# Square feed-forward layers as seven half-size products instead of eight

## The chip, the cores and the metric

The kernel runs on one core of a Trainium2 chip. Its time is the device time of one execution in microseconds (us); three runs of the kernel before gave 1289.44, 1290.35 and 1290.55, so the median is 1290.35. The core has TensorE (PE: matmuls, with PEld for its weight loads), VectorE (DVE), ScalarE (ACT), GpSimd (POOL) and SyncE (SP), each with its own queue of instructions that it runs in order; semaphores join them. SBUF is the on-chip memory, PSUM the small memory into which TensorE accumulates, in banks of 128 x 512 fp32.

## The reference

A transformer block on x of shape (4, 1024, 256), all fp32. Cut to what matters:

```
x = x + layernorm(attention(layernorm(x)))          # 16 heads of 16
n = layernorm(x)
h = silu((n @ w1.T) * s1) * ((n @ w2.T) * s2)       # 256 -> 1024, the gated layer
h = gelu((h @ h1.T) * t1)                           # 1024 -> 1024, square
h = gelu((h @ h2.T) * t2)                           # 1024 -> 1024, square
x = x + layernorm((h @ w3.T) * s3)                  # 1024 -> 256, the last layer
```

The weights of the feed-forward part hold only -1, 0 and 1, with one scale per output. The activations are fp32. The kernel keeps that accuracy by splitting each activation into a high part that TensorE's faster fp32r form represents exactly and a low part, the rest; the weights are exact in that form, so a product takes two matmuls, one for each part.

## The kernel before

The program is written with its order by hand: the order in which Python records instructions is the order in each engine's queue. `tile_fast` first runs attention for the four batches. Its main loop (`while weighed < len(tiles)`, L1015) records score matmuls (L473), exponentials on ScalarE (L474) and weighted sums (L481), and between them calls `side.take()`. `Side` (L606) holds chains of `Step`s, each with a gap in slots and a flag for whether it uses TensorE; one `take` is one slot, in which every chain's next due steps are recorded, at most one of them on TensorE. Normalisations, transposes, projections, loads, and the rounding of weights are such steps.

`round_weights` (L246) has GpSimd load a block of weights, cast it to fp32r and write it back to DRAM; 22 blocks in all, 16 of them of h1 and h2. Later `load_weights` (L757) brings h1 into eight tiles that the attention's stacks held (`homes["h1"]`), and h2 and w3 into tiles that come free with the attention. They stay there for the whole feed-forward stage.

`feed_forward` (L947) goes over eight half batches of 512 tokens. For each:

- `gated` (L818): per block of 128 outputs eight matmuls (`pg`, L816), SiLU on ScalarE (L830), the product on VectorE (L832), a split into high (ScalarE, L820) and low (VectorE, L821), and a `side.take()` every second block.
- `gelu_layer` (L840), once for h1 and once for h2: per pair of output blocks, 32 matmuls (`ph`, L816) over eight input blocks, with a `side.take()` after every second one; then GELU (ScalarE, L852), the high part (VectorE, L853) and the low part (VectorE, L854).
- `finish` (L856): the last layer (`pz`, L869) and a chain of side steps that normalises, adds x and stores. VectorE normalises (`Norms.apply`, L114); GpSimd computes the reciprocal root (`Norms.root`, L106). For the last half batch this is recorded in place and not as side steps.
- `prepare` (L784): side steps that normalise and transpose the next half batch's rows.

`check_weights` and `count` (L918) load the weights again and compare them with the rounded ones, in 44 pieces of 128 x 512; `judge` (L932) sums the misses with a small matmul, and if there are any, the slower `tile_general` runs. PSUM is used as three pairs of banks (`ps`, tag `big`), one bank for the attention's sums and one (`misc`) for small work.

## Time and profile before

| what | us |
|---|---|
| median of three runs | 1290.35 |
| the profiled execution, its own time | 1287.27 |
| its span, first to last instruction | 1285.4 |
| TensorE busy in the span (96%) | 1237.9 |
| VectorE busy (57%) | 728.2 |
| ScalarE busy (54%) | 699.9 |
| GpSimd busy (9%) | 121.3 |
| first `pg` matmul of the feed-forward stage, from the span's start | 611.36 |

Matmuls are pipelined and their ends are modelled, so TensorE's busy time counts overlaps: a `ph` matmul reads as 390 ns, while the next starts about 227 ns after it. How often matmuls start is what counts. Groups are given by line, engine, operation and tile, with busy time, mean length of one, and the idle time of the engine just ahead of them with what ended it.

### The profile page before, as it was taken

To read this page: it belongs to the slowest core of one execution; us is meant where nothing else is said; L and a number is where in the kernel's file an instruction comes from. 1 tells how busy PE (TensorE), PEld (TensorE's weight loads), DVE (VectorE), ACT (ScalarE), POOL (GpSimd) and SP (SyncE) were. 2 spreads that over 40 slices of the span, in tenths; PEclk is the share of its full clock that TensorE was granted. 3 is DMA by queue.
4 is the path that set the end of the run, shared out by engine and by line. 5 is a ranking of instruction groups with operands and counts; after the bars stand their busy time and mean duration, and the time that the engine had idled before them with its cause. 6 is when DMAs were issued, how large, how long until landed. Compare 5 with 4: busy or idle time off the path is not lost.

```text
span 1285.4 us, 21095 instructions
## 1 busy us (share of the span) xinstructions
PE 1237.9 (96%) x8104; PEld 767.9 (60%) x8104; DVE 728.2 (57%) x1625; ACT 699.9 (54%) x855; POOL 121.3 (9%) x166
## 2 busy tenths in 40 slices
PE   7999999999999999998999999999999999999995
PEld 3333333333333334333788888888888888888885
DVE  3566566865677647655653635538356374463533
ACT  4788788888888888998412414214132141331410
POOL 6211021110111110000000000000000000000000
PEclk9999999999999999999999999999999999999998
DMA  5776654566465654563310000201102011020000
GB/s 139 175 181 164 152 121 133 117 159 145 117 165 120 152 136 79 100 161 111 133 62 1 25 1 1 74 17 42 49 1 71 20 42 49 1 67 9 17 1 20
DMA packets 65679, 107.03 MB, mean 83 GB/s; under 512 B 12960, under 2 KB 39200, under 8 KB 65568
## 3 DMA queue, kind: packets, MB, share of 16 engines
q1 hardware_dynamic: 57680, 80.93, 25.4%
q0 software_dynamic: 7360, 24.12, 6.1%
q8 instruction: 66, 1.08, 0.3%
q10 hardware_dynamic: 528, 0.52, 0.1%
q14 instruction: 45, 0.37, 0.1%
HBM read 48.38 MB, written 23.59 MB: 56 GB/s over the span
## 4 chain that ended last, share of the span: by engine, by line
PE 75%; DVE 8%; ACT 8%; DMA 3%; issue 3%; SPq 1%; ACTq 1%; POOL 0%; POOLq 0%; DVEq 0%
PE ph L816 36%; PE acc L481 12%; PE s L473 8%; ACT e L474 6%; PE pz L869 4%; PE pg L816 4%; PE p L267 4%; PE py L267 2%; DVE sg L832 2%; PE pv L267 2%; DVE top L490 1%; DVE ha_lo L821 1%; DVE st L96 1%; PE po L520 1%; SPq L421 1%
## 5 line engine op out<-in xcount | busy, mean ns | idle before, releaser
L474 ACT ACTIVATE e<-s 128x1024 f32<-128x1024 f32 x512 | 482.9, 1037 | 53.7 <-PE s L473 43.8
L481 PE MATMUL acc<-e,vaug 128*32 128x512 f32 x2048 | 255.1, 600 | 2.4 <-POOL vaug L451 2.3
L852 ACT ACTIVATE a<-ph,h_scale 128x512 f32<-128x512 f32 x128 | 81.3, 688 | 301.1 <-PE ph L816 301.1
L473 PE MATMUL s<-sq,sk 64*128 64x512 f32 x1024 | 184.7, 441 | 17.1 <-ACT e L474 13.5
L816 PE MATMUL ph<-hb_hi,h 128*128 128x512 f32 x512 | 199.5, 390 | 0.0
L816 PE MATMUL ph<-hb_lo,h 128*128 128x512 f32 x512 | 199.4, 389 | 0.0
L473 PEld LDWEIGHTS s<-sq,sk 64*128 64x128 f32 x1024 | 85.5, 184 | 137.3 <-ACT e L474 115.0
L490 DVE TENSOR_TENSOR top<-top,e 128x512 f32<-128x512 f32 x192 | 134.9, 702 | 16.0 <-ACT e L474 10.9
L106 POOL TENSOR_TENSOR rstd<-ve,minus_half 128x4 f32<-128x4 f32 (+1 forms) x33 | 38.4, 1162 | 831.5 <-DVE ve L104 831.5
L481 PEld LDWEIGHTS acc<-e,vaug 128*32 128x32 f32 x2048 | 49.1, 108 | 106.9 <-issue 101.8
L816 PEld LDWEIGHTS ph<-hb_hi,h 128*128 128x128 f32 x512 | 96.1, 188 | 20.2
L816 PEld LDWEIGHTS ph<-hb_lo,h 128*128 128x128 f32 x512 | 96.1, 188 | 20.1
L853 DVE CAST ha_hi<-a 128x512 fp32r<-128x512 f32 x64 | 27.1, 423 | 142.7 <-ACT a L852 142.7
L816 PE MATMUL ph<-ha_hi,sq 128*128 128x512 f32 x256 | 101.8, 398 | 0.4
L816 PE MATMUL ph<-ha_lo,sq 128*128 128x512 f32 x256 | 99.8, 390 | 0.0
L816 PE MATMUL ph<-ha_lo,sk 128*128 128x512 f32 x256 | 99.7, 390 | 0.0
L816 PE MATMUL ph<-ha_hi,sk 128*128 128x512 f32 x256 | 99.7, 389 | 0.0
L830 ACT ACTIVATE sg<-pg,w_scale 128x512 f32<-128x512 f32 x64 | 43.4, 690 | 55.9 <-DVE ha_lo L821 45.4
L832 DVE SCALAR_TENSOR_TENSOR sg<-pg,w_scale,sg 128x512 f32<-128x512 f32 x64 | 47.1, 745 | 46.3 <-ACT sg L830 46.2
L267 PE MATMUL p<-xT,wqk_sb 128*32 128x512 f32 x512 | 61.9, 602 | 6.3 <-ACT wqk_sb L194 2.6
L853 DVE CAST hb_hi<-a 128x512 fp32r<-128x512 f32 x64 | 27.0, 422 | 71.5 <-ACT a L852 71.5
L816 PEld LDWEIGHTS ph<-ha_hi,sq 128*128 128x128 f32 x256 | 48.1, 188 | 13.0 <-DVE sg L832 3.4
(165 smaller groups left out, 1636.7 us busy)
## 6 DMA issues: line engine op xcount, KB each, us to landing
w<-in_h_dram POOLq DMA_DIRECT2D x16, 512.0 KB, 5.7
h_r<-wr POOLq DMA_DIRECT2D x16, 512.0 KB, 3.9
x<-in_h_dram SPq DMA_DIRECT2D x32, 256.0 KB, 2.7
top_d<-top SPq DMA_DIRECT2D x30, 256.0 KB, 2.3
folded<-top_d SPq DMA_DIRECT2D x30, 256.0 KB, 3.1
sk<-ck1hi SPq DMA_DIRECT2D x64, 64.0 KB, 2.7
sk<-ck1lo SPq DMA_DIRECT2D x64, 64.0 KB, 3.0
sq<-cq1hi SPq DMA_DIRECT2D x64, 64.0 KB, 2.5
```

Of the source, the lines that this page charges most:

```text
L106: nc.gpsimd.tensor_tensor(rstd[:, :n], ve[:, :n], self.minus_half[:, :n], ALU.pow)
L267: nc.tensor.matmul(o[j : j + SLOT, :], w[:, j : j + SLOT], i, **flags)
L473: nc.tensor.matmul(s[:, a, :], stacks[1, g % 2, u][r, c * P : (c + 1) * P], stacks[0, g % 2, u][r, h * NQ : (h + 1) * NQ], start=True, sto ...
L474: nc.scalar.activation(pair(k)[:, u], s, AF.Exp)
L481: nc.tensor.matmul(acc[SLOT * i : SLOT * (i + 1), :], vaug[g % 2][:, c, i, :], pair(k)[:, i // 2, i % 2, :], start=c == 0, stop=c == NT - 1)
L490: nc.vector.tensor_max(top, top if c > 1 else pair(k - 2)[:, :, :, 0:P], pair(k)[:, :, :, 0:P])
L816: nc.tensor.matmul(p, homes[n][c][:, m * P : (m + 1) * P], half[:, c, :], start=c == 0 and k == 0, stop=c == len(homes[n]) - 1 and k == 1)
L830: nc.scalar.activation(sg, p[:, 0, :], AF.Silu, scale=scales["w1"][:, m : m + 1])
L832: nc.vector.scalar_tensor_tensor(sg, p[:, 1, :], scales["w2"][:, m : m + 1], sg, ALU.mult, ALU.mult)
L852: nc.scalar.activation(a, p[:, j, :], AF.Gelu, scale=scales[n][:, m : m + 1])
L853: nc.vector.tensor_copy(o[0][:, m, :], a)
L869: nc.tensor.matmul(p[t], half[:, c, t * P : (t + 1) * P], homes["w3"][c], start=c == 0 and k == 0, stop=c == HC - 1 and k == 1)
```

## The change

The square layers are now computed for a whole batch (two halves of 512 tokens) by a scheme with seven products of half-size blocks. The weight is a 2 x 2 array of blocks, the activation another (upper or lower 512 features, first or second 512 tokens), and seven products of sums and differences give the four output blocks.

- *Weight side.* `round_corners` takes the place of `round_weights` for h1 and h2: GpSimd copies three corners and forms four sums or differences, and stores seven "factors" per layer to DRAM. `load_factor` brings one factor (1 MB) at a time into a ring of four slots, which are the tiles that held h1.
- *Activation side.* `Operand` splits a block into high (now a ScalarE copy of 128 x 1024) and low (VectorE). `t1`, `make2`, `make3`, `make4` form sums of operands on VectorE.
- *A layer.* `Layer.run` records 14 groups of 16 matmuls, seven products with two pairs of row blocks each. Where one product serves several sums, the partial sum is copied by ScalarE from one pair of PSUM banks to another (`branch`) or to SBUF (`keep_copy`), and matmuls go on accumulating on the copy. Side steps, splits and sums stand in a table by group (`steps`).
- *Around it.* `gated` runs both halves of a batch, 16 blocks, without splits of its own and with a `side.take()` at each; its last steps split and add the first operands of the layer after. `finish` handles both halves. ScalarE normalises (`Norms.scale`, `Norms.shift`) rows of batches after the first and the endings of all batches but the last. The check compares whole blocks of 128 x 1024 with an int8 copy that ScalarE makes, in 22 pieces, and `judge` is recorded just before the last batch's `finish`. The first batch's second half is prepared during attention.

```diff
+    def shift(self, stats, n=TPQ):
+        mv, rstd = stats
+        nb = self.small.tile([P, TPQ], F32, tag="nb", name="nb")
+        self.nc.vector.scalar_tensor_tensor(nb[:, :n], mv[:, :n, 0], -1.0, rstd[:, :n], ALU.mult, ALU.mult)
+        return rstd, nb
+
+    def scale(self, o, t, shifted, i):
+        rstd, nb = shifted
+        self.nc.scalar.activation(o, t, AF.Identity, bias=nb[:, i : i + 1], scale=rstd[:, i : i + 1])
...
+        def round_corners(n, c, x):
+            def load():
+                st["w"] = work.tile([P, WIDE], F32, tag="w", name="w", bufs=1)
...
+                for j in range(2):
+                    nc.gpsimd.dma_start(out=st["w"].rearrange("p (j i n) -> p j i n", j=2, i=2)[:, j], in_=rows[:, j])
...
+            def plain():
+                r = work.tile([P, WIDE], F32R, tag="wr", name="wr", bufs=1)
+                nc.gpsimd.tensor_copy(r[:, 0:half], st["w"][:, 0:half])
+                nc.gpsimd.tensor_copy(r[:, half : 3 * half], st["w"][:, 2 * half : 4 * half])
+                store(r, 0, 3)
+
+            def sums():
+                r = work.tile([P, WIDE], F32R, tag="wr", name="wr", bufs=1)
...
+                nc.gpsimd.tensor_tensor(s1, a21, a22, ALU.add)
+                nc.gpsimd.tensor_tensor(s2, s1.bitcast(F32), a11, ALU.subtract)
+                nc.gpsimd.tensor_tensor(s3, a11, a21, ALU.subtract)
+                nc.gpsimd.tensor_tensor(s4, a12, s2.bitcast(F32), ALU.subtract)
+                store(r, 3, 7)
...
+            return [Step(load, 2, False), Step(plain, 3, False), Step(sums, 1, False)]
...
+        order = (0, 1, 4, 5, 2, 3, 6)
+        def load_factor(q):
...
+            n, k = square[q // len(order) % 2], order[q % len(order)]
+            for i, t in enumerate(ring_of[q % SLOTS]):
+                nc.sync.dma_start(out=t.bitcast(F32), in_=factors[n][k, :, 2 * i : 2 * i + 2, :].bitcast(F32))
...
+            def high(self, i):
+                self.hi[i] = Half("hi", F32R)
+                nc.scalar.copy(self.hi[i].t, self.raw[i].t)
+
+            def low(self, i):
+                self.lo[i] = Half("lo", F32R)
+                nc.vector.tensor_sub(self.lo[i].t, self.raw[i].t, self.hi[i].t.bitcast(F32))
...
+            def run(self, q, scale, extra):
...
+                steps = {
+                    0: [hi(2, 0), self.t1(1), self.make2(1), lo(2, 0)],
+                    1: [hi(2, 1), lo(2, 1), self.make4(0), self.make4(1)],
+                    2: [self.make3(0), self.make3(1), hi(3, 0), lo(3, 0)],
+                    3: [hi(3, 1), lo(3, 1)] + take,
+                    4: [hi(4, 0)] + take + [lo(4, 0)],
...
+                    9: [hi(6, 1)] + take + [lo(6, 1)],
+                    10: take, 11: take,
+                }
...
+                def products(k, r, start):
+                    p = at[r]
+                    for c in range(HC // 2):
+                        for j in range(2):
+                            w = ring_of[(q + k) % SLOTS][c // 2][:, c % 2, (2 * r + j) * P : (2 * r + j + 1) * P]
+                            for n, half in enumerate(self.moving[k].pairs(c)):
+                                nc.tensor.matmul(
...
+                    if r:
+                        self.moving[k].release()
+                        load_factor(q + k + SLOTS)
+
+                def add(n, i, j, r):
+                    o = out[n][r]
...
+                    nc.vector.tensor_add(o.t, at[r], o.t)
+                    gelu(o, i, r)
+
+                def keep_copy(n, r):
...
+                    nc.scalar.copy(o.t, at[r])
...
+                def branch(r):
+                    first[r] = at[r]
+                    nc.scalar.copy(space(r), first[r])
...
+                space(0), products(0, 0, True), branch(0), after(0)
+                space(1), products(0, 1, True), after(1)
+                second(0), branch(1), after(2)
+                products(2, 0, False), keep_copy("u", 0), after(3)
+                second(1), after(4)
+                products(2, 1, False), keep_copy("u", 1), after(5)
+                for g in range(6, 14):
+                    k, r = g // 2, g % 2
...
+                    if k == 3:
+                        keep_copy("w", r)
+                    elif k == 4:
+                        straight(1, r, at[r])
+                    else:
+                        add(*(("w", 1, 1) if k == 5 else ("u", 0, 1)), r)
+                    after(g)
...
+                steps = {g: [side.take] for g in range(NH * HC)}
+                for g, runs in (
+                    (7, opened + split(corner, 0)), (8, split(corner, 1)), (10, split(low, 0)), (11, split(low, 1)),
+                    (12, [one.t1(0)]), (13, [one.make2(0)]), (14, []), (15, []),
+                ):
...
+                two.run(q + 7, scales["h2"], extra)
+                until(lambda: not chain[0])
+                quiet[0] = False
+                if last:
+                    side.flush()
+                    side.add(judge())
+                    side.flush()
+                chain = finish(b, ops, {0: split(ops[0, 1], 0) + split(ops[0, 1], 1)}, [Step(check, 0, False)] if b == 0 else [])
```

## The prediction

> **What bounds the kernel now.** The page comes first: the span, the busy tenths and the granted clock.
>
> ```profile
> span 1285.4 us, 21095 instructions
> ...
> PE   7999999999999999998999999999999999999995
> ...
> DVE  3566566865677647655653635538356374463533
> ACT  4788788888888888998412414214132141331410
> ...
> PEclk9999999999999999999999999999999999999998
> ```
>
> TensorE is 90% busy or more in nearly every slice, at full clock. ScalarE is as busy as TensorE up to slice 20 (the attention, with its exponentials) and idle for most of the second half; VectorE has room throughout. A busy TensorE is not yet a limit, so the chain that ended last, in order of time, is next, over one steady half batch of the feed-forward stage:
>
> ```profile
> 782.61 3.67 PE pg L816 x16
> ...
> 797.32 14.80 PE ph L816 x64
> 812.56 1.86 PE ph L816 x8
> 814.85 41.79 PE ph L816 x184
> 856.64 7.67 PE pz L869 x64
> 864.31 3.67 PE pg L816 x16
> ```
>
> From one `pg` to the next is 81.70 us: 14.71 for the gated layer (64 matmuls), 59.32 for the two square layers (256 matmuls and eight small transposes), 7.67 for the last layer. A matmul in the long run costs 41.79 / 184 = 0.227 us. The groups by form give what the other engines pay:
>
> ```profile
> L474 ACT ACTIVATE e<-s 128x1024 f32<-128x1024 f32 x512 | 482.9, 1037 | 53.7 <-PE s L473 43.8 <-DVE top L490 4.1 <-ACT e L474 2.4
> L852 ACT ACTIVATE a<-ph,h_scale 128x512 f32<-128x512 f32 x128 | 81.3, 688 | 301.1 <-PE ph L816 301.1
> L832 DVE SCALAR_TENSOR_TENSOR sg<-pg,w_scale,sg 128x512 f32<-128x512 f32 x64 | 47.1, 745 | 46.3 <-ACT sg L830 46.2
> L854 DVE TENSOR_TENSOR hb_lo<-a,hb_hi 128x512 fp32r<-128x512 f32 x64 | 44.3, 692 | 2.3
> ```
>
> The GELU (L852) waits for TensorE, not the reverse. So removing matmuls from the square layers shortens the kernel one for one, as long as nothing else gets late. A window of the transfers at the start of the feed-forward (GB/s is the last column) bounds what weight loads can reach:
>
> ```profile
> 640.00:644.00 4.00, 4.00 (x19) 3.32 (x18) 2.43 (x7) 1.27 (x2) 0.00 (x0) 1.00 1.02 414
> ```
>
> **The Trainium skill.** *ScalarE: Activation LUTs*, "What ACT_TABLE_LOAD costs", has an activation at 186 ns + 0.833 ns per element and about 93 ns for each pointer operand. It gives 1039 ns for 1024 elements; the trace has 1037 (L474). *VectorE: DVE Perf Modes*, "The TRN2 errata", has an fp32 tensor_tensor at (N+151)/0.96 ns: 691 for 512, where the trace has 692. *PSUM — Partial Sum Buffer*, "The four PSUM rules", says that writes by ScalarE leave the accumulate bits alone, so a matmul without the first-flag adds to such data where matmuls have written the bank before. The change rests on this; the kernel before never does it, so no trace here shows it. *GPSIMD Engine Reference*, 3.1, has a two-input add at about twice VectorE's time.
>
> **The change, part by part.**
>
> *Matmuls.* Before, a batch (two halves) takes 2 x 256 = 512 matmuls in the square layers. After, a layer is 7 products x 2 row pairs x 16 = 224, so 448 per batch. Removed: 4 x 64 = 256, times 0.227 = **-58.1**. Nothing on TensorE hides that, since it is the chain. The period of 81.70 is 0.5 more than its parts (320 x 0.227 + 7.67 + 0.88 for transposes = 81.2); such seams come half as often: **-2**. The gated and last layers keep their 512 matmuls each.
>
> *Work beside a layer.* A layer now has 14 groups of 3.63 us, 50.8 us. ScalarE, all priced from L474 and L852: 14 splits, 4 kept copies and 2 branch copies at 1.04, 16 GELUs at 0.64 (back to back): 31 us. VectorE: 14 low parts, 8 sums of operands, 4 adds at 1.2 (the skill's 1.22, less overlap): 31 us. With normalisation and checks both stay under 80%, so rates fit and only hand-overs can cost. I followed them in the order of the built program. Branch copy of row pair 0: starts at 3.8, done 4.9, wanted at 7.25. Of row pair 1: behind two GELUs that start at 11.0, done 13.4, wanted at 14.5; queued behind it on ScalarE are splits wanted only at 21.8. The third product wants its last low part at 10.9: t1 and its difference for half 1, then a split and two subtractions, done at about 8.5. These cost nothing, with 1 to 2.5 us of cover.
>
> Two do not fit. The second `w` add of product 6 stands on VectorE behind a low part whose split stands on ScalarE behind two GELUs and four normalisations (0.49 each by the skill's rule with two pointers) or two check casts (1.04 each): done near 47.8 to 48.3, wanted at 47.15. That is 0.7 in three layers and 1.2 in one. With checks at a layer's end the next layer's operand sums start late by some 3 us, and the third product waits up to 2, in three batches: I take 1. Sum **+6**, bounds 0 and 20.
>
> *Gated layer.* Splits, sums and the previous batch's two endings now go into 16 steps of 1.82 us, so VectorE has 26 of 29 us to do. Where statistics and low parts coincide (steps 6 to 12) it falls about 3.5 us behind; the three PSUM buffers give 1.9 of cover (two groups, 3.64, less 1.7 for SiLU and product). 1.5 in three batches, 0.5 in the first: **+5**, bounds 0 and 14.
>
> *Weight factors.* They come from DRAM for each product, 56 loads of 1 MB, two DMAs each on SP's queue. A product lasts 32 x 0.227 = 7.27 us, so 144 GB/s is needed; the window shows 414. A load is issued when its ring slot's product ends and used three products later (22 us); check loads ahead of it on SP may hold it for some 5 us. Cost 0; without that cover it is the second rival below.
>
> *Making the factors.* GpSimd did one 1147 ns cast per block; now two copies and four adds of 256 (0.56 each by the skill's ratio, without start), and two loads and two stores. The second half of a block waits for the first's store (3.9 us to landing before), because one buffer serves both. Behind it in GpSimd's queue stand `rstd` and `vaug`; VectorE waits for `rstd`. TensorE's order in attention is the same up to the last 16 groups. In two places an `rstd` follows closely. **+2**, bounds -1 (a gain is excluded but for the few transposes moved) and 10.
>
> *End.* The final check's matmul now stands between the last product and the last layer, behind an add and a reduction: **+1.8**. In the last batch both halves are normalised in place. The timeline of the end before shows what a block of two tiles costs VectorE:
>
> ```profile
> 1268.43 0.76 DVE L871 TENSOR_TENSOR z<-pz,w3s_sb 128x256 f32<-128x256 f32 x2 [0.72 <-PE pz L869]
> ...
> 1272.91 0.74 DVE L871 TENSOR_TENSOR z<-pz,w3s_sb 128x256 f32<-128x256 f32 x2
> ...
> 1277.04 0.43 DVE L877 TENSOR_TENSOR z<-z,x 128x256 f32<-128x256 f32 x1
> ```
>
> 4.5 us a block against 3.84 of TensorE. Four blocks and two low parts end at 4.0 + 2.4 + 18.1 = 24.5 after the first `pz`, 9.1 after TensorE's last; before it is 5.2. **+4**.
>
> Sum: -58.1 - 2 + 6 + 5 + 2 + 1.8 + 4 = -41.3. On the profiled execution's 1287.27 (span 1285.4 and 1.9 around it) that is 1246.0; the median of the runs shown, 1290.35, is 3.1 above that execution, so **1249**. A difference under 0.2%, 2.6 us, can't be told from none.
>
> **Rivals.**
>
> *All hidden* (chance 0.15). If the hand-overs fit and attention stays, only the check's matmul and the end remain: -60.1 + 5.8 = -54, 1236. For it: both engines have a quarter of their time free. Against: the two places above are late by their order, whatever the mean.
>
> *VectorE and ScalarE set the pace* (0.15). In-order queues can turn 80% load into a late hand-over in most groups. 0.2 us in each of 112 groups is 22 us more: 1271. For it: one late split passes on to adds, GELUs and the next split, across both engines. Against: most steps have over 1 us of cover each 3.6 us, so lateness is worked off.
>
> *The factor stream is late* (0.07), the one that ends slower. Everything saved is gone at 42 us / 56 = 0.75 us more per product, that is at 8.0 us a load or 131 GB/s; at 115 GB/s a product takes 9.1 us and the time is 1249 + 56 x 1.85 = 1353. For it: all loads pass one queue in order, behind stores and checks that wait. Against: 414 GB/s in the window, and 22 us of lead.
>
> *It doesn't do what it says* (0.02): if accumulation onto copied sums needed other matmuls, the count would not fall, and the time is about 1290.
>
> **How the numbers follow.** The main case has 0.61, with its own range 1241 to 1258. Leaving out the lowest tenth (under 1236, most of "all hidden" lies above it) and the highest (beyond 1267: the slower case and the worse part of the pace case) gives 1236 to 1267. Faster: 0.61 + 0.15 + 0.14 = 0.90; within 0.2%: 0.02; slower: 0.08.
>
> **What would show it.** 1792 `ph` matmuls at 0.227, no group of low parts above 1.25, a batch from gated layer to gated layer of 150 to 152 us against 163.4, and 9 us of VectorE after the last `pz`. Idle TensorE on `ph` put down to VectorE adds means the hand-overs, and above 20 us the pace rival; put down to DMA of factors, the stream. The attention ending more than 5 us later than at 611 would make my GpSimd term wrong.

## The result: 1286.7 us for 1289.2

The changed kernel takes 1286.66 us (median of 12 runs, 1283.73 to 1292.07) beside 1289.17 us for the kernel before (12 runs, 1286.14 to 1290.95): a ratio of 0.9985, 95% interval 0.9972 to 0.9999; 0.15%, under the 0.2% that can be told from no change. The prediction was 1249, so of 41 us of expected gain 39 are missing. The profiled execution took 1288.74 us, with a span of 1287.0; before it was 1287.27 and 1285.4.

The matmuls did go. From the page of the changed kernel, the span, the busy times, the granted clock in 40 slices and the chain that ended last; then one of the four groups of `ph` matmuls:

```profile
span 1287.0 us, 20876 instructions
...
PE 1206.6 (94%) x7848; PEld 727.2 (57%) x7848; DVE 823.9 (64%) x1454; ACT 883.0 (69%) x1043; POOL 209.2 (16%) x279
...
PEclk8999899999999999999999999999999999999997
...
PE 60%; ACT 15%; DVE 15%; issue 5%; SPq 2%; DMA 2%; POOL 1%; ACTq 0%; POOLq 0%; DVEq 0%
...
L1014 PE MATMUL ph<-hi,sq 128*128 128x512 f32 x448 | 178.5, 398 | 8.7 <-DVE g L936 5.6
```

4 x 448 = 1792 `ph` matmuls, 256 fewer, as the change says. The chain that ended last read like this on the page of the kernel before:

```profile
PE 75%; DVE 8%; ACT 8%; DMA 3%; issue 3%; SPq 1%; ACTq 1%; POOL 0%; POOLq 0%; DVEq 0%
```

TensorE's share went from 75% to 60%, those of VectorE and ScalarE from 8% to 15% each. Time has moved from multiplying to waiting for one of the other two. TensorE's waits from the first square layer to the end (engine and line, what it waited for, us in total, times, longest):

```profile
PE pn L1187 <- DVE total L1183: 6.6, 1, 6.6
PE fpt L873 <- ACT fxn L123: 5.6, 15, 2.1
PE ph L1014 <- DVE g L936: 5.6, 4, 1.8
PE pz L1121 <- ACT hi L903: 3.4, 3, 1.3
PE ph L1014 <- DVE w L1025: 2.9, 4, 1.3
PE pz L1121 <- DVE lo L907: 2.6, 3, 0.9
PE pg L933 <- DVE g L936: 2.4, 3, 0.8
...
```

Seven kinds (an eighth, of 0.2 us, is left out), few of each, none over 7 us: no single bottleneck, but hand-overs that come late. There are no waits for the weight factors' DMAs among them.

A ledger closes the sum. It takes the distance between the starts of successive matmuls from the first `pg` to the last `pz` in each trace, less what such a matmul takes when nothing is in the way (0.2267 us for `ph` and `pg`, 0.120 for `pz`, 0.108 for a transpose), and sorts the excess by where it falls.

| us, whole feed-forward | before | after | difference |
|---|---|---|---|
| 256 `ph` matmuls at 0.2267 | | | -58.0 |
| `ph` matmuls further apart than 0.2267, with no wait | 1.6 | 9.4 | +7.8 |
| matmuls stretched by a half TensorE clock | 0 | 6.4 | +6.4 |
| waits inside the last layer (`pz`) | 0 | 8.1 | +8.1 |
| the wait for the weight comparison (`pn`) | 0 | 6.8 | +6.8 |
| waits at the transposes (`fpt`) | 0 | 9.0 | +9.0 |
| waits in and behind the gated layer | 1.5 | 10.3 | +8.8 |
| waits between `ph` groups | 0 | 4.4 | +4.4 |
| attention's last projections inside the first gated layer | 0 | 2.0 | +2.0 |
| sum (the rest is under 0.5) | | | -4.7 |

The feed-forward is 4.7 us shorter, the attention in this profile 4.8 longer (the first `pg` at 616.1 after 611.3), and from the last `pz` to the end it takes 1.5 more: 1.6 us more of span. The next three views show how such waits arise.

**Inside the last layer.** Batch 2, first TensorE, then the queues it waits for (start, duration, engine, line, operation; in brackets the idle time before and what ended it):

```profile
935.47 0.28 PE L1121 MATMUL pz<-w_sb,lo 128*128 128x256 f32 x1
937.03 0.38 PE L1121 MATMUL pz<-w_sb,hi 128*128 128x256 f32 x1 [1.28 <-ACT hi L903]
938.29 0.39 PE L1121 MATMUL pz<-w_sb,lo 128*128 128x256 f32 x1 [0.88 <-DVE lo L907]
...
939.80 0.42 PE L1121 MATMUL pz<-w_sb,hi 128*128 128x256 f32 x1
940.02 0.42 PE L1121 MATMUL pz<-w_sb,lo 128*128 128x256 f32 x1
```

```profile
931.18 2.36 DVE L907 TENSOR_TENSOR lo<-w,hi 128x1024 fp32r<-128x1024 f32 x2 [2.34 <-ACT hi L903]
933.46 1.22 DVE L1025 TENSOR_TENSOR u<-ph,u 128x1024 f32<-128x1024 f32 x1
934.59 0.68 DVE L1126 TENSOR_TENSOR z<-pz,w3s_sb 128x512 f32<-128x512 f32 x1
937.01 2.36 DVE L907 TENSOR_TENSOR lo<-u,hi 128x1024 fp32r<-128x1024 f32 x2 [1.74 <-ACT hi L903]
```

```profile
934.71 1.34 ACT L1002 ACTIVATE u<-u,h_scale 128x512 f32<-128x512 f32 x2 [2.62 <-DVE u L1025]
935.95 1.97 ACT L903 CAST hi<-u 128x1024 fp32r<-128x1024 f32 x2
```

The last product had ended at 928.0. Its second add (`u`, 933.46) stands on VectorE behind two low parts of `w`, which wait for their high parts on ScalarE. From the add follow GELU, high part and low part, and the second half of the last layer starts with exactly this block. TensorE has 7.7 us of work for the first half (64 `pz` matmuls) and needs 2.6 more. After the wait the `pz` matmuls start 0.22 us apart instead of 0.12. The windows of the first two batch ends show the granted clock (us, busy of PE, PEld, DVE, ACT and POOL, granted clock, DMA share, GB/s):

```profile
770.00:775.00 5.00, 3.49 (x28) 3.09 (x26) 3.26 (x4) 3.28 (x5) 0.00 (x0) 1.00 0.00 0
775.00:780.00 5.00, 4.72 (x27) 4.72 (x28) 1.96 (x3) 1.22 (x1) 0.00 (x0) 0.66 0.00 0
...
938.00:943.00 5.00, 4.71 (x26) 4.59 (x27) 1.97 (x3) 1.23 (x1) 0.00 (x0) 0.66 0.01 3
```

A clock of 0.66 over 5 us is 3.4 us at one half, and in these 3.4 us 1.1 to 1.6 us of work are lost.

**At the end of the gated layer.** Batch 2, ScalarE and then VectorE:

```profile
808.23 0.69 ACT L935 ACTIVATE sg<-pg,w_scale 128x512 f32<-128x512 f32 x1 [0.19 <-PE pg L933]
813.02 2.08 ACT L123 ACTIVATE z<-z,nb,rstd 128x256 f32<-128x256 f32 x4 [4.10 <-DVE nb L118]
815.01 1.24 ACT L935 ACTIVATE sg<-pg,w_scale 128x512 f32<-128x512 f32 x2
```

```profile
812.83 0.16 DVE L118 SCALAR_TENSOR_TENSOR nb<-mv,rstd 128x4 f32<-128x4 f32 x1 [0.24 <-POOL rstd L108]
...
815.71 0.75 DVE L936 SCALAR_TENSOR_TENSOR g<-pg,w_scale,sg 128x512 f32<-128x512 f32 x1 [1.58 <-ACT sg L935]
```

The four normalisations of the batch before (`z`) stand in ScalarE's queue ahead of the SiLUs (`sg`). ScalarE is idle for 4.1 us, with two SiLUs behind it that could run; VectorE waits for the SiLU, and TensorE for VectorE, because the SiLU products free the PSUM buffers (0.95 us inside the last groups, 1.9 before the first `ph`).

**At the transposes.** ScalarE and TensorE in batch 2:

```profile
862.82 1.33 ACT L1002 ACTIVATE w<-w,h_scale 128x512 f32<-128x512 f32 x2 [2.43 <-DVE w L1025]
864.05 2.06 ACT L123 ACTIVATE fxn<-x,nb,rstd 128x256 f32<-128x256 f32 x4
```

```profile
862.23 0.40 PE L1014 MATMUL ph<-lo,sk 128*128 128x512 f32 x1
864.69 0.33 PE L873 MATMUL fpt<-ident,fxn 128*128 128x128 f32 x1 [2.06 <-ACT fxn L123]
865.18 0.33 PE L873 MATMUL fpt<-ident,fxn 128*128 128x128 f32 x1 [0.16 <-ACT fxn L123]
```

Here the normalised inputs (`fxn`) stand behind two GELUs that wait for an add. TensorE's queue is in order too: all the `ph` matmuls behind the four transposes wait with them.

### The profile page after: what moved, and what is told of

Same layout as the page of the kernel before. It is cut to its first block, busy times and chain, and to the rows that moved or that the text cites. A ratio compares the mean times of both kernels' runs of the same rounds, so it can differ in the third digit from the quotient of the medians.

```text
span 1287.0 us, 20876 instructions
## 1 busy us (share of the span) xinstructions
PE 1206.6 (94%) x7848; PEld 727.2 (57%) x7848; DVE 823.9 (64%) x1454; ACT 883.0 (69%) x1043; POOL 209.2 (16%) x279
## 3 DMA queue, kind: packets, MB, share of 16 engines
q8 instruction: 64, 1.05, 0.3%
## 4 chain that ended last, share of the span: by engine, by line
PE 60%; ACT 15%; DVE 15%; issue 5%; SPq 2%; DMA 2%; POOL 1%; ACTq 0%; POOLq 0%; DVEq 0%
PE ph L1014 22%; PE acc L536 12%; PE s L528 8%; ACT e L529 6%; PE p L322 4%; PE pg L933 3%; DVE lo L907 3%; ACT hi L903 3%; PE pz L1121 3%; PE py L322 2%; SPq L476 2%; DVE g L936 2%; DVE top L545 2%; PE pv L322 1%; ACT w L1002 1%
## 5 line engine op out<-in xcount | busy, mean ns | idle before, releaser
L1014 PE MATMUL ph<-hi,sq 128*128 128x512 f32 x448 | 178.5, 398 | 8.7 <-DVE g L936 5.6
L1014 PE MATMUL ph<-lo,sq 128*128 128x512 f32 x448 | 176.5, 394 | 0.0
L1014 PE MATMUL ph<-hi,sk 128*128 128x512 f32 x448 | 176.3, 394 | 0.0
L1014 PE MATMUL ph<-lo,sk 128*128 128x512 f32 x448 | 176.3, 394 | 0.0
L1014 PEld LDWEIGHTS ph<-hi,sq 128*128 128x128 f32 x448 | 84.2, 188 | 32.5 <-DVE g L936 7.3
L1014 PEld LDWEIGHTS ph<-hi,sk 128*128 128x128 f32 x448 | 84.0, 188 | 19.9
L1014 PEld LDWEIGHTS ph<-lo,sk 128*128 128x128 f32 x448 | 84.1, 188 | 19.8
L1014 PEld LDWEIGHTS ph<-lo,sq 128*128 128x128 f32 x448 | 84.1, 188 | 18.8
L1121 PE MATMUL pz<-w_sb,hi 128*128 128x256 f32 x256 | 67.8, 301 | 3.4 <-ACT hi L903 3.4
L1121 PE MATMUL pz<-w_sb,lo 128*128 128x256 f32 x256 | 67.8, 301 | 2.6 <-DVE lo L907 2.6
```

What stands on the lines that cost most here:

```text
L1014: nc.tensor.matmul(p[:, j, :], w, half, start=start and c == n == 0, stop=c == HC // 2 - 1 and n == 1, skip_group_check=True,)
L1121: nc.tensor.matmul(p[:, j, :D], half[:, (t0 + j) * P : (t0 + j + 1) * P], homes["w3"][c], start=c == n == 0, stop=c == HC - 1 and n == 1,)
```

## The experiments

My theory after the traces: late hand-overs at four places, each with its own remedy, and a half clock that follows from some of them. The rival: VectorE and ScalarE have too much work, so that a wait taken away comes back elsewhere. "Work theory" below is this rival.

| run | median us | ratio to the kernel before, 95% |
|---|---|---|
| changed kernel | 1286.66 | 0.9985 (0.9972 to 0.9999) |
| e1, sums of operands after the gated layer | 1283.80 | 0.9951 (0.9936 to 0.9966) |
| e2, transposes later | 1280.47 | 0.9926 (0.9901 to 0.9950) |
| e3, end of a batch reordered | 1271.38 | 0.9862 (0.9847 to 0.9877) |
| e4, these three | 1263.37 | 0.9796 (0.9779 to 0.9813) |
| e5, `z` normalised later | 1287.03 | 0.9979 (0.9968 to 0.9990) |
| e6, normalising on VectorE | 1271.36 | 0.9862 (0.9835 to 0.9889) |
| e7, e4 and e5, comparison last | 1263.74 | 0.9798 (0.9780 to 0.9816) |
| e9, operands on the weights' alignment | 1279.89 | 0.9930 (0.9908 to 0.9953) |
| e10, the best of all | 1251.33 | 0.9702 (0.9676 to 0.9728) |
| e14, kernel before with 96 bytes moved | 1298.04 | 1.0068 (1.0044 to 1.0091) |

e8, e11, e12 and e13 were run once each, for their traces: 1285.19, 1287.67, 1287.35 and 1289.08 us.

**e1: sums of operands after the gated layer.**

```diff
-                    (12, [one.t1(0)]), (13, [one.make2(0)]), (14, []), (15, []),
...
+                emit([one.t1(0), one.make2(0)])
```

> One edit: the first layer's two sums of operands (t1 and the difference for row pair 0) are issued after the gated layer instead of in its steps 12 and 13. Hand-over theory (VectorE is behind at the end of the gated layer, so its products with the SiLU leave PSUM late, and TensorE waits 0.95 us inside the last groups and 1.9 us before the first ph, in each batch): both gaps fall under 0.4 us in every batch, 4 x 2.5 = 10 us less than the changed kernel's 1286.7, so 1277 (1274 to 1280). Work theory (VectorE and ScalarE have too much to do, so a wait taken away here comes back): the same sum of gaps turns up before the third product of the first layer, and the time is 1285 to 1287.

The gaps of 0.95 and 1.92 us stayed in batches 2 to 4 to within 0.04 us; only in the first batch, which has no ending to normalise, did the 0.45 us before `ph` go. The feed-forward took 655.9 us after 656.2; what the median gained lies elsewhere, since the attention of this profile ended 3 us earlier. So VectorE's sums were not what ended last there; that they count once ScalarE is out of the way shows in e10. It was this miss that sent me to ScalarE's queue and the 4.1 us of idle time shown above.

**e2: transposes two side steps later.**

```diff
-                + [Step(transposes(c), 1 if c or b else 2) for c in range(DC)]
+                + [Step(transposes(c), 1 if c else 3 if b else 2) for c in range(DC)]
```

> One edit: the transposes of a half's normalised inputs come two side steps later after the normalising. Hand-over theory (the transposes are issued into TensorE's queue right behind the normalising on ScalarE, which itself stands behind splits and GELUs): the waits before and between the fpt transposes, 1.6, 3.8 and 3.6 us in the first three batches, go, and 8 us with them: 1279 (1276 to 1282). Work theory: the transposes pile up at the end of the second layer, and 1286 stays.

All 9.0 us at the transposes went. The waits between `ph` groups grew from 4.4 to 7.6; the transposes' copies and low parts now stand before other splits, which is the likely reason but was not tried. A third came back, two thirds stayed.

**e3: the end of a batch.** The last add goes ahead of the low parts of the lower right block, the second half of the last layer takes that block first, and the comparison's sum goes between the blocks of the last layer.

```diff
-                extra[12] = split(ops[1, 1], 0) + split(ops[1, 1], 1)
+                extra[12] = [lambda i=i: late.high(i) for i in range(2)]
+                extra[13] = [lambda i=i: late.low(i) for i in range(2)]
+                late = ops[1, 1]
...
-                        i, d = c // (HC // 2), c % (HC // 2)
+                        i, d = c // (HC // 2) ^ h, c % (HC // 2)
...
+                    if b == B - 1 and h and not t0:
+                        side.add(judge())
+                        side.flush()
```

> Two edits at the end of a batch. VectorE does the last add of product 7 before the low parts of the lower right block, and the second half of the last layer contracts over its lower block first. The final count of the weight comparison goes between the last layer's blocks. Hand-over theory with the clock (the two waits of 1.1 to 1.4 us inside the last layer of each batch set off one window of 3.4 us at half the TensorE clock): the waits of 2.2, 2.8 and 2.8 us and the half-clock windows at the ends of batches 1 to 3 (1.6, 1.3 and 1.1 us of stretched matmuls) go, and 4 to 5 of the 6.8 us before the last layer of batch 4: 16 us, 1270.5 (1267 to 1275); no half-clock window between 150 us and 1240 us. If the low clock has another cause, the windows stay at the same places and the time is 1275. Work theory: the waits move to the second half's first matmuls in full and it is 1283 or more.

The waits inside the last layer are gone in batches 1 to 3, and with them the half clock at these places. The windows of this run at the ends of batches 1 and 2:

```profile
770.00:775.00 5.00, 5.00 (x45) 5.00 (x45) 0.92 (x2) 0.00 (x0) 0.00 (x0) 1.00 0.00 0
...
928.00:933.00 5.00, 5.00 (x44) 5.00 (x43) 1.92 (x3) 0.48 (x1) 0.00 (x0) 1.00 0.00 0
```

One half-clock window is left in the middle, at 1017, right behind the transposes' wait. What I had wrong was the comparison: its matmul waited 6.5 us between the blocks as before it had waited 6.8 ahead of them, because its sum stood on VectorE behind the low parts and then behind the endings of the last layer's first two blocks, from 1240.9 to 1249.3. While TensorE waited, VectorE did work that had stood at the end: from the last `pz` to the end it is now 10.6 us instead of 15.0. So 4.4 us came from a place that the expectation did not name, and that its number was nearly met, 1271.4 for 1270.5, is in this part luck.

**e4: the three together.**

> The three edits before together. Hand-over theory: the gains add, 10 + 8 + 16 = 34 us: 1253 (1248 to 1258), with TensorE waits inside the feed-forward under 8 us in all and a batch of 151 to 153 us. Work theory: VectorE and ScalarE become the limit once the first waits are gone, and no more than half adds: over 1268. What stays against the predicted sum is the ph matmul at 0.2315 instead of 0.2267 us (9 us) and the attention (5 us).

23 us of 34. Missing are the 10 that e1 did not bring; the other two add in full.

**e5: `z` normalised later.**

```diff
-                + [Step(apply(i), 0 if i else gap, False) for i in range(0, TPQ, 2)]
+                + [Step(apply(i), 0 if i else 3, False) for i in range(0, TPQ, 2)]
```

> One edit: in the ending of a batch the four normalisations of z on ScalarE are issued three side steps after the statistics instead of one (first half: two). Theory after the first runs (the z normalisations wait at the head of ScalarE's queue for VectorE's statistics, and the SiLUs of the gated layer stand behind them; that is the 0.95 + 1.92 us that TensorE waits at the end of the gated layer in batches 2 to 4): these gaps fall under 0.4 us, 8 us less than 1286.7: 1278.5 (1276 to 1281). If VectorE's own backlog holds the SiLU products, the gaps stay.

The gaps of the gated layer fell from 2.9 to 1.9 us a batch, but the endings finished later, the next inputs with them, and 3.1 us of waits between `ph` groups took the place of 1.7 in batch 2 and 3.5 of 0.7 in batch 3. In sum nothing: for this one edit it went as the work theory has it.

**e6: normalising back on VectorE.** `norms.scale` becomes `norms.apply` in both places, and `norms.shift` goes.

> One part of the change undone: inputs and endings are normalised on VectorE, as before the change, at the same steps. Hand-over theory: the gap at the end of the gated layer (2.9 us in batches 2 to 4) and most of the waits at the fpt transposes (9 us in all) go, since neither SiLUs nor transposes stand behind a queue of ScalarE any more: 1273 (1269 to 1278). Work theory (VectorE was short of time, which is why ScalarE was given the work): VectorE's 5 us more per batch turn up as waits of TensorE on adds and low parts: 1290 or more.

15 us faster. ScalarE's queue no longer holds an operation that waits for VectorE's statistics and GpSimd's root: at the transposes 1.8 us are left of 9.0, in and behind the gated layer 7.3 of 10.3, and the half clock costs 1.9 instead of 6.4 (in this profile; where its stretches fall is chance, see the last section). The part of the change that gave ScalarE the normalising cost most of this time by itself. The edit also takes 25 us of work off ScalarE (12.5 for `z`, 12.4 for `fxn`), so it doesn't alone tell the order of a queue from its load; e3, which moves no work between engines, does. Two of the 15 us have another source: without the small `nb` tiles the left pool (one of two that share SBUF from opposite ends; the operands lie in both) moved by 96 bytes, and the `ph` matmuls came closer together (7.4 us of excess, not 9.4); e9 shows why that can be.

**e7: all edits so far, the comparison's matmul behind the last product.**

> All edits together: sums after the gated layer, transposes two steps later, the reordered end of a batch, z normalised later, and the weight comparison's sum and matmul behind the last layer's products. Hand-over theory: 1263.4 of the three edits less 8.5 (gated layer) less 4.5 of the 6.5 us before pn (the rest stays as a wait for the last low parts): 1250 (1246 to 1255), batches 2 and 3 at 153 us. Work theory: over 1259.

The same as e4. The gated layer gained its 2 us, the transposes of batches 2 and 3 waited 3.6 and 2.1 us again and each wait was followed by a half-clock window. At the end TensorE finished earlier than in e4, but VectorE with the endings of the last four blocks only 2.9 us earlier, and from its last instruction to the end of the kernel it was 8.8 us instead of 5.6; e10 shows why.

**e8: what the distance of the `ph` matmuls depends on.** Without any wait they are 0.2315 us apart on average, 0.2272 before. The trace speaks against the transfers at once: in the last products of the last batch, where no factor is loaded any more, it is 0.231 to 0.233. Each layer of this kernel changes one thing:

```diff
+                    v = q // len(order)
...
+                    if v == 3:
+                        pairs_of.sort(key=lambda at: at[1])
...
+                            if v == 1:
+                                w = ring_of[(q + k) % SLOTS][0][:, 0, 0:P]
+                            if v in (5, 7):
+                                w = homes["w1"][c % 2][:, (2 * r + j) * P : (2 * r + j + 1) * P]
+                            moving = self.moving[k].pairs(0 if v == 4 else c)
+                            if v == 2:
+                                moving = [moving[0]] * 2
+                            if v in (6, 7):
+                                moving = [t[:, c % 2, :] for t in x_in[0]]
```

> Leaves the right result out; only the distance between ph matmuls counts, layer by layer. Layer 1: as changed. 2: every matmul reads one and the same weight block of its ring slot. 3: the high part twice, no low part. 4: all matmuls of one PSUM bank first, then the other's. 5: always the first chunk of the operand. 6: weights from the gated layer's tiles. 7: operands from the gated layer's tiles. 8: both from there. Address theory (weights or operands lie where TensorE reads them slower): 0.2315 falls to 0.2267 in layer 6 or 2 (weights), in 7, 5 or 3 (operands), and in 8 surely. Order theory (a group of 8 matmuls in each of two banks): 0.2267 in layer 4 alone. Neither: 0.231 to 0.232 in all eight, 8 too, and the cause lies in how the groups hand over.

Mean distances in ns, layers 1 to 8: 232.8, 232.3, 231.6, 232.3, 230.3, 232.5, 227.3, 226.9. Only operands from the gated layer's tiles bring 0.227 back. In layer 5, where one pair of operands stays for 16 matmuls, the addresses in the built program sort the pairs: both in the left pool 0.227 to 0.228 once settled, one in each pool 0.230, both in the right pool 0.234. The tiles of the left pool and the weights both begin 896 bytes above a multiple of 1024, those of the right pool 992.

**e9: 96 bytes of padding.**

```diff
+                if k == 0:
+                    nc.gpsimd.memset(ffn["fb"].tile([P, 24], F32, name="pad"), 0.0)
```

> The changed kernel with 96 unused bytes at the end of the pool on the right, so that all operands begin at the same byte modulo 1024 as the weights (before, those of the right pool began 96 bytes further on; those of the left pool at the same byte). Address theory (in the profile of the changed kernel, ph matmuls with both operands in the left pool are 0.227 apart once settled, with one in each 0.230, with both in the right pool 0.233 to 0.234): all 1792 at 0.227, 4 x 2.2 = 9 us less: 1277.7 (1275 to 1281). If the pools differ for another reason, 0.2315 and 1286.7 stay.

All eight layers are at 0.2267 to 0.2274 now, and the excess falls from 9.4 to 1.2 us. Four matmuls of the changed kernel with both operands in the right pool, then four of this one:

```profile
821.27 0.39 PE L1014 MATMUL ph<-hi,sq 128*128 128x512 f32 x1
821.50 0.40 PE L1014 MATMUL ph<-lo,sq 128*128 128x512 f32 x1
821.74 0.39 PE L1014 MATMUL ph<-hi,sq 128*128 128x512 f32 x1
821.97 0.39 PE L1014 MATMUL ph<-lo,sq 128*128 128x512 f32 x1
```

```profile
821.01 0.39 PE L1014 MATMUL ph<-hi,sq 128*128 128x512 f32 x1
821.23 0.39 PE L1014 MATMUL ph<-lo,sq 128*128 128x512 f32 x1
821.46 0.39 PE L1014 MATMUL ph<-hi,sq 128*128 128x512 f32 x1
821.69 0.39 PE L1014 MATMUL ph<-lo,sq 128*128 128x512 f32 x1
```

Each distance differs by a hundredth of a microsecond at most; over 1792 of them the excess is 8 us less. The median fell by 7.

**e10: the best of it.** The normalising of e6, the reordered end of e3 with the comparison behind the last product, the sums of e1, and operands on the weights' alignment.

> Normalising back on VectorE, the reordered end of a batch, the weight comparison's sum and matmul behind the last layer, sums after the gated layer, and operands at the same byte modulo 1024 as the weights. From the 1271.4 of normalising on VectorE: waits inside the last layer 2.3 + 2.6 + 2.5 gone, the last batch's end 6 shorter, 0.5 in the first gated layer, ph matmuls 0.2267 (7.3): 1250 (1246 to 1254). If the parts share their gain, 1258 or more.

1251.3 us, 3% under the kernel before. Batches 2 and 3 take 153.0 and 151.9 us. What TensorE still waits for from the first square layer on:

```profile
PE pn L1189 <- DVE total L1185: 6.2, 1, 6.2
PE ph L1012 <- DVE w L1023: 3.8, 4, 1.5
PE ph L1012 <- DVE u L1023: 0.8, 2, 0.4
PE fpt L871 <- DVE fxn L127: 0.7, 1, 0.7
...
```

In the gated layer the sums of e1 now matter. VectorE's queue at the end of that layer in batch 2, first in e6, then here:

```profile
806.21 1.38 DVE L127 TENSOR_SCALAR z<-z,mv,rstd 128x256 f32<-128x256 f32 x4 [0.24 <-POOL rstd L108]
807.51 1.22 DVE L917 TENSOR_TENSOR g<-g 128x1024 f32<-128x1024 f32 x1
808.64 0.75 DVE L934 SCALAR_TENSOR_TENSOR g<-pg,w_scale,sg 128x512 f32<-128x512 f32 x1
```

```profile
803.49 1.38 DVE L127 TENSOR_SCALAR z<-z,mv,rstd 128x256 f32<-128x256 f32 x4 [0.24 <-POOL rstd L108]
804.79 0.74 DVE L934 SCALAR_TENSOR_TENSOR g<-pg,w_scale,sg 128x512 f32<-128x512 f32 x1
```

In e6 a sum of operands (`g<-g`) stands ahead of the SiLU product that frees a PSUM buffer, and TensorE waits 1.47 us before the first `ph` in batches 2 to 4; here it waits 0.33. From e5, which has the sums in the old place, to e7, which has them behind, the same wait of 1.12 us goes too. So two late hand-overs stood one behind the other: e1 took away the second while the first was still there, and saw nothing.

The first line of the waits is no wait of later matmuls any more, as this matmul is TensorE's last, but its new place has a price. It gives the flag `bad`, which all five engines load and branch on before the kernel can close. In the changed kernel the flag was there 27 us before VectorE's last instruction. Here it is VectorE's last instruction:

```profile
1241.20 0.14 DVE L1190 CAST bad<-pn 1x1 int32<-1x1 f32 x1
```

TensorE's branch, which takes 3.4 to 4.0 us in all 16 profiles and elsewhere ends before VectorE does, runs only now, from 1241.97 to 1245.53. From VectorE's last instruction to the end it is 8.6 us (8.8 in e7, which has the same order), against 5.5 to 5.7 in the changed kernel, e3, e4 and e6. So 3 us of TensorE's gain are lost to the flag, and an order that has both was not tried. Another 1.6 us are VectorE's: with the four endings of the last batch it ends 10.8 us after the last `pz`, 9.2 in the changed kernel. Together they make the 19.7 us from the last `pz` to the end, where the changed kernel has 15.0.

**e11 and e12: the attention.** e11 leaves the sums of weights out; e12 is the kernel before once more.

> Leaves the sums of weights out: GpSimd copies where it added, one instruction of 1024 elements for four of 256 (the factors are then wrong, and so is the result). Only the attention counts: the time from its first to its 1920th acc matmul, 548.7 us in the changed kernel and 546.0 before. If GpSimd's adds lengthen the attention, 546 to 547; if it is the stores and loads of twice the number, or windows of half clock that come by chance, 547.5 to 550.

> The kernel before, once more, for a second profile. If the half-clock windows near 140 us belong to the change, there is none here either, and the first to the 1920th acc matmul take 546.0 +- 0.5 us; if they come by chance, one may appear and cost up to 1.7 us each.

From the first `acc` matmul to the one 1920 further on e11 took 550.3 us, the changed kernel 548.7, so the sums are not seen to lengthen the attention. e12 took 547.3 after 546.0, and had a half-clock window at 139 us, which the first profile of this kernel had not. Over the twelve profiles of kernels with the changed attention as it is (e11 apart) the way from the first `acc` to the first `pg` is 581.3 to 585.9 us, median 582.5; in the three with the attention of before (e14 below is one) it is 579.9, 581.2 and 582.8. By the medians the change lengthens the attention by 1.3 us. Single profiles of one kernel differ by more, since windows of half clock come by chance, and three profiles of the attention before are too few to tell this from nothing.

**e13 and e14: which addresses, and is it the change?** e13 puts 32 unused bytes behind each operand buffer of the right pool; e14 puts 96 between operands and weights of the second square layer in the kernel before.

> The changed kernel with 32 unused bytes behind each of the right pool's 14 operand buffers, so that their distance to the weights differs by 32 bytes from one to the next. If it is only the difference modulo 64 that counts, the even buffers are at 0.227 and the odd ones slow; if modulo 128, every fourth is at 0.227; if any difference counts, only the pairs at 0 modulo 512 are at 0.227 and all others at 0.230 to 0.234.

> The kernel before, with 96 unused bytes between the operands and the weights of the second square layer in the pool on the right; nothing else differs. Address theory: its 1024 ph matmuls are 0.233 apart instead of 0.227, 6 to 7 us more than 1289: 1295.5 (1293 to 1298), while the first square layer stays at 0.227. If the slower matmuls belong to the change, the time stays.

e14 settles the second question: the first square layer stays at 0.2273, the second goes from 0.2271 to 0.2343, and the time from 1288.3 to 1298.0, the upper end of what was expected. Of these 9.7 us 7.3 are in the feed-forward (first `pg` to last `pz` 668.0 us after 660.7); the rest is not explained. Three of its matmuls:

```profile
838.59 0.40 PE L817 MATMUL ph<-hb_lo,h 128*128 128x512 f32 x1
838.82 0.40 PE L817 MATMUL ph<-hb_hi,h 128*128 128x512 f32 x1
839.05 0.39 PE L817 MATMUL ph<-hb_lo,h 128*128 128x512 f32 x1
```

So it is the addresses, with nothing of the change in it, and it is the difference that counts, not the address. In the built program the second layer's operands now begin at 896 and its weights at 992; unmoved, both are at 992, and in the first layer both are at 896, at 0.227 each time. e13 leaves the exact rule open, but is nearest to the last of its three readings. Pairs with both differences at 0 modulo 512 have a median of 0.227, and most others 0.229 to 0.235, with 0.230 where one difference is 256 or 384; each pair stays for 8 matmuls only, and the distance needs about as many to settle. Why the difference matters was not found.

## Why the prediction was wrong

The arithmetic of its steps is right; what failed are the sizes of some terms and what was left out. The largest miss is a term that it put at nothing: the hand-over into the last layer and the half clock that follows, 14.5 us. By its own steps, with the ledger's numbers:

- **Matmuls, -58.1.** The count was right. The duration was not: 0.227 was taken over from other buffers, and the change moves operands to buffers 96 bytes off the weights' alignment. Measured 0.2315; +7.8. This term was mis-sized, and e9 and e14 show the cause.
- **Seams, -2.** Measured 0: what the ledger leaves beside its rows, the small gaps at the heads of layers among it, is 9.8 us before and 10.3 after.
- **Hand-overs inside layers, +6 (0 to 20).** The late `w` add was there: 4.4 us between `ph` groups, 1.5 at the worst. But I counted ScalarE's four normalisations only as something that delays the add, and never asked who waits for them. The transposes do, and 9.0 us with them. In sum 13.4, inside the bounds.
- **Gated layer, +5 (0 to 14).** Measured 8.8, and 2.0 for the attention's last projections. The wait that ended last was not the one in the prediction. I had VectorE behind with low parts; in the trace ScalarE is idle behind a `z` that waits, and taking 2.4 us of work from VectorE alone changed nothing there (e1). VectorE's lateness was real but hidden, and came from the sums: once ScalarE's wait was gone, they were worth 1.1 of the 2.9 us a batch (e6 and e10, e5 and e7).
- **Factor stream, 0.** Right; no wait of TensorE for these loads.
- **Making the factors, +2 (-1 to 10).** 1.3 by the medians, within what was said, but not told from nothing. GpSimd's adds took 0.81 to 0.97 us, not the 0.56 of the prediction, without harm. The 4.8 of the one profile contain 1.9 before the first `acc`, which varies from 30.0 to 34.0 us with the half clock at the start.
- **The comparison's matmul, +1.8.** Measured 6.8. I priced the add and the reduction, but not the place of the reduction in VectorE's queue, behind the last two low parts of `w` and the last add.
- **End, +4.** VectorE took 9.2 us after the last `pz` (9.1 predicted, 5.2 before), so the mechanism was right. Yet the end is only 1.5 later: what lies between VectorE's last instruction and the end was 7.9 us before and 5.5 now. GpSimd's closing drain takes 6.3 us in the three profiles with the attention of before and 3.2 in the thirteen others; why was not tried.
- **Not in the sum at all:** the hand-over into the last layer, 8.1 us, and the half clock, 6.4. I followed the order of the square layers product by product and stopped at their end, with "the gated and last layers keep their 512 matmuls each". They do, but the last layer's operands now come out of the last product by a chain of add, GELU, high and low part. Before, most of it was split while the square layer still ran. And the clock stood at 1.00 in nearly all of the profile before, so I took it for a constant.

Added up, with the attention as this profile has it, these misses come to 43 us, which is what lies between a predicted gain of 41.3 and a span 1.6 longer.

Of the rivals, "VectorE and ScalarE set the pace" is nearest, but not as I priced it: 0.2 us in each of 112 groups. The lost time sits in some ten places per batch, where one in-order queue stands behind an operation that waits for another; e3 gets 15 us back by order alone, and e6 as much by giving the normalising back to VectorE. With the places mended the time comes near the prediction: e10's batches 2 and 3 take 152 to 153 us, against 150 to 152 predicted, and the kernel 1251, against 1249. But e10 is another kernel, with less of the waits that the prediction had counted in and a longer end, so that the two numbers meet is in part chance.

The Trainium skill's statement in *PSUM — Partial Sum Buffer*, "The four PSUM rules", that ScalarE's writes leave the accumulate bits alone, fits the trace as far as a trace can tell: there is no matmul more than the 1792, so the second products need no others to bring the copied sums in. A trace shows no values. The prices from *ScalarE: Activation LUTs* and *VectorE: DVE Perf Modes* held as well (`hi` 1.05 us, `lo` 1.224). What was wrong on ScalarE and VectorE was not the price of an instruction, but who stands behind whom.

## What to carry to other kernels

When a change removes work from the engine that is the bound, follow each new operand up to every consumer, the stages that "stay the same" included, and for each operation that is moved to another engine's in-order queue ask what it waits for and what stands behind it; that both engines were busy under 80% of the time told nothing of either here. When an edit that should free an engine changes nothing, a second wait may stand in front of it (e1): try it again when that one is gone. A wait of 2.2 to 2.6 us on TensorE cost up to 1.6 more here, because a half clock may follow. Where a buffer moves, compare the distance of the matmuls after it with that before: a difference in start address between weights and operands cost 2 to 3% of their pace here with no wait to see.

## What the runs showed of the hardware

**The half clock comes in fixed stretches.** The trace's clock records give 1 or 0.5 only, in stretches of 3.413 us or multiples, on one grid through a whole execution. *TensorE: Matmul & The Clock Gate* in the Trainium skill, "What's actually happening", tells of a free-running window of 3413 ns and of a clock that is halved after an idle window. The window agrees, 3.413 us in the records. But the stretch ahead need not be idle. In the feed-forward of these 16 profiles, taking as busy what a matmul needs by the ledger, all 30 full-clock stretches with TensorE under 0.385 busy were followed by half clock, 5 of 36 between there and 0.475, and none above. So a wait of 2.3 us costs a stretch if it falls into one stretch of the grid, and nothing if it straddles two. The changed kernel has both: the waits inside the last layer of batch 2 fell into the stretch before 939.3, which left it 0.29 busy, and half clock followed; the wait before the transposes at 864.69, 2.2 us by the ledger, fell into two stretches, 0.50 and 0.48 busy, and no half clock came. e6 has the same waits of 2.3 to 2.6 us inside the last layer in batches 1 to 3, and no half clock after them. Where the grid lies against the start of the kernel differs from profile to profile, so a kernel with such waits varies: of the four runs of e6 the fastest took 1268.04 us at a mean clock of 0.992, the slowest 1275.33 at 0.985.

**Start addresses of operands and weights.** Matmuls of 128x512 in fp32r follow each other at 0.2267 to 0.2274 us if weights and operands begin at the same byte modulo 512, at 0.230 if one of two alternating operands begins 96 bytes off, and at 0.233 to 0.234 if both do (e8, e9, e14), each once it has settled over some 8 matmuls. Within a weight tile the blocks begin 512 bytes apart, and in the kernel before the pace is the same for each.

**The branch at the end.** TensorE's branch on the flag took 3.4 to 4.0 us in all 16 profiles; it is hidden as long as the flag is there early, and 3 us of it show when the flag comes last (e7, e10).
